# Seven quarter products in place of eight for two sequences' slot sums, in an attention and soft-mixture kernel

## The chip, the cores and the metric

The kernel runs on one core of a Trainium2 chip. The metric is the device time of one execution in microseconds (us). Three runs of the kernel before took 662.78, 663.25 and 664.02 us; their median, 663.25 us, is the time before.

## The reference, cut to what matters

The input x has 4 sequences of 2048 tokens with 256 channels, all in float32. The first half is a causal linear attention (no softmax over scores) with a two-layer MLP for each of q, k and v, a layer norm, a residual and another layer norm. The second half, which the change touches, is a soft mixture of experts with 16 experts of 16 slots, so 256 slots:

```python
logits = jnp.einsum('bnd,des->bnes', x_unit * scale, mu_unit)
dispatch = jax.nn.softmax(logits, axis=1)                  # over the 2048 tokens
combine = jax.nn.softmax(logits.reshape(B, N, E * S), axis=-1).reshape(B, N, E, S)
slot_in = jnp.einsum('bnd,bnes->besd', xn, dispatch)       # the slots' sums
h = jax.nn.gelu(jnp.einsum('besd,edh->besh', slot_in, w1) + b1[None, :, None, :], approximate=False)
slot_out = jnp.einsum('besh,ehd->besd', h, w2) + b2[None, :, None, :]
out = jnp.einsum('besd,bnes->bnd', slot_out, combine)
```

For one sequence, `slot_in` is a product of a 256 x 2048 matrix (slots by tokens, the exponentials of the logits) and a 2048 x 256 matrix (tokens by channels), divided by each slot's sum of exponentials. A column of ones beside the 256 channels yields that sum, so the product's second factor is 257 wide.

## The kernel before, in words

The 8192 tokens are cut into 16 groups of 512 (`W`), four to a sequence; a group lies in SBUF as 128 partitions by 4 chunks by channels. The work of group t is in four parts: `attend(t)` (q, k, v, scores, running state; from L776 on), `norms(t)` (the two layer norms, xn, its squares; L1022), `back(t)` (logits, their row softmax, a running smallest value `mx`, since the logits are kept with the opposite sign; L1141) and `finish(t)` (the combination with the slots' outputs, the last norm, the store; L1450). After the last group of each sequence come `softmaxes` (the largest logit of each slot is found, spread over all partitions and subtracted, then exponentials; L1234) and `slots` (the slots' sums, the experts' MLP; L1338). The last sequence is treated apart, its first three groups ahead of its last.

In `softmaxes` the way from `mx` to a tile `dg` that holds each slot's largest logit on all partitions is: two transposes on TensorE (L1246), a reduce on VectorE (L1254, tile `cm`), and `spread`, that is two VectorE instructions that make diagonal matrices (L677), one matmul of ones by the diagonals (L683) and a copy by ScalarE (L1271). GpSimd then subtracts (L1282) and ScalarE takes exponentials (L1294).

In `slot_sums` (L1316) 16 matmuls, one for each chunk of 128 tokens, accumulate one half of the slots by 257 columns in a PSUM bank of tag `ps_at`; two halves make 32 matmuls for a sequence. `slots` takes the reciprocal of the last column (L1353) and scales (L1354), and goes on with transposes (L1368), the first expert layer (L1392), transposes (L1411), a gelu and the second layer (L1438). `finish` multiplies by the slots' outputs `so` (L1542).

x comes in twice: as rows (tile `row`, L315) and, from group 2 on, also by blocks of 32 x 32 straight from memory (tile `xT`, eight DMAs, L338), which a VectorE transpose of 32 x 32 blocks then turns (L787). For groups 0 and 1 TensorE transposes `row` instead (L486, eight transposes), and VectorE and ScalarE copy the results (L476, L477).

The order of instructions on each engine is fixed before the launch by a planner, `Plan.run`: each step has an estimated length, a rank (set by `plan.begin(t + something)`), and its readers and writers; the planner takes, again and again, the step that can begin earliest by its own estimates, with the delays of `LATE` between engines. Places in SBUF, PSUM and memory are given out by tag, with a fixed count for each tag. Every engine executes its list in that order, and waits where a step's input is not there yet. SyncE (SP) issues nearly all DMAs, in one list. PSUM has 8 banks: three of tag `mm`, two of `tp`, three of `at`.

Of the kernel before, what the change touches and what calls it, by code (L numbers as in the profile page):

```python
# [17 lines left out]

PIECES = ((2, False), (2, True))

CENTERS = [['ACT', 'ACT', 'ACT', 'ACT'], ['ACT', 'DVE', 'DVE', 'DVE'], ['ACT', 'ACT', 'ACT', 'ACT'], ['DVE', 'DVE', 'DVE', 'DVE'], ['ACT', 'DVE', 'ACT', 'DVE'], ['ACT', 'DVE', 'DVE', 'DVE'], ['ACT', 'ACT', 'ACT', 'ACT'], ['DVE', 'DVE', 'ACT', 'DVE']]

SUBTRACT = ['DVE', 'POOL', 'DVE', 'POOL']

TAIL = {'norms': 0, 'back': 0.3, 'softE': 1.4, 'part': 2.2, 'soft': 1.0, 'slots2': 4.6, 'fin2': [5.5, 0.3], 'slots3': 1.7, 'fin3': [2.6, 0.2], 'table': 1.0}
LAST = 2
W = G * P
# [27 lines left out]

class Plan:

    LATE = {"PE": 0.45, "DVE": 0.25, "ACT": 0.25, "POOL": 0.25, "SP": 3.5, "IN": 0.0}
    TABLE = 1.3

    PATIENCE = {"PE": 0.0, "DVE": 0.0, "ACT": 0.0, "POOL": 0.0, "SP": 1.0, "IN": 0.0}
# [19 lines left out]
        self.order[tag].append(b)  # L81
        return b

    def step(self, engine, length, emit, reads=(), writes=(), table=None, holds=()):


        s = Step(engine, length, emit, self.base + self.count, table)
        s.holds = list(holds)
        for b in holds:
            b.left += 1  # L90
        self.count += 0.01

        if any((a[0] if isinstance(a, tuple) else a).tag.startswith("ps_") for a in reads):
            s.rank -= 1.5
        for accesses, write in ((reads, False), (writes, True)):
            for a in accesses:
                b, parts = a if isinstance(a, tuple) else (a, range(a.parts))
                if b not in s.buffers:
                    s.buffers.append(b)
                    b.left += 1  # L100
                for p in parts:
                    s.before.update(b.writers[p])
                    if write:
                        s.before.update(b.readers[p])
        for accesses, write in ((reads, False), (writes, True)):
            for a in accesses:
                b, parts = a if isinstance(a, tuple) else (a, range(a.parts))
                for p in parts:
                    if write:
                        b.writers[p], b.readers[p] = [s], []  # L110
                    else:
                        b.readers[p].append(s)
        s.before.discard(s)
        s.waiting = len(s.before)
        for o in s.before:
            o.after.append(s)
        self.steps.append(s)

    def run(self):
# [25 lines left out]
        while left:  # L145
# [43 lines left out]
                    since[b.tag].append(b.last)  # L189
            for o in s.after:  # L190
                o.waiting -= 1
                seen = end + (self.LATE[e] if o.engine != e or e == "SP" else 0.0)
                o.ready = max(o.ready, seen)
                if not o.waiting:
                    ready[o.engine].append(o)
# [4 lines left out]
def _act(n, pointers=0):  # L200
    return 0.16 + 0.00083 * n + 0.093 * pointers


def _dve(n):
    return 0.155 + 0.00105 * n
# [6 lines left out]
def _pe(n):  # L212
    return max(0.22, 0.00168 * n)
# [6 lines left out]
def kernel(  # L220
# [43 lines left out]
    for tag, n, shape in (  # L264
# [3 lines left out]
        ("kT", 1, [KC, W]),  # L268
        ("vt", 1, [G, C]),
        ("kt", 1, [G, C + 1]),  # L270
        ("sT", 1, [G, P]),
        ("a", 2, [G, C]),
        ("run", 2, [C]),
# [3 lines left out]
        ("xnT", 1, [KC, W]),  # L277
        ("lg", 7, [G, ES]),
        ("mx", 1, [ES]),
        ("ct", 5, [EH, W]),  # L280
        ("dg", 1, [EH, P]),
        ("si", 1, [EH, C]),
        ("siT", 1, [KC, ES]),
# [13 lines left out]
    plan.tag(  # L297
        "bounce", [memory.tile([KC, W, P], F32, name=f"bounce_{i}") for i in range(16)], True
    )
    plan.tag("sums", [memory.tile([G, C], F32, name=f"sums_{i}") for i in range(2)], True)  # L300
    bank_places("mm", 3)
    bank_places("tp", 2)
# [5 lines left out]
    def load_x(t):  # L308
# [14 lines left out]

        plan.step("SP", {0: 2.5, 1: 6.0, 2: 4.0}.get(t, 0.5), emit, writes=[xt])
        x_tiles[t] = xt
        if t < 2:
            return


# [907 lines left out]
    def softmaxes(groups, before=None):  # L1237
# [22 lines left out]
        if before:  # L1260
# [3 lines left out]
                nc.vector.tensor_tensor(less.place, cm.place, before.place, ALU.subtract)  # L1264

            plan.step("DVE", 0.3, emit, [before], [cm, less])
        row = spread(cm)
        cmb = plan.buffer("dg")
        plan.step(
            "ACT", _act(ES),  # L1270
            lambda: nc.scalar.copy(cmb.place.rearrange("p h e -> p (h e)"), row[:, :ES]),  # L1271
            [row], [cmb],
        )
        for t in groups:

            n = 1 if t == ngroups - 1 else G
# [30 lines left out]
    def slot_sums(groups, h):  # L1307
# [13 lines left out]
            plan.step("PE", _pe(C + 1), emit, [(l_tiles[t], [c]), n_tiles[t][0]], [psi])  # L1321
        return psi

    def part_sums(groups):

        kept = plan.buffer("xT", KC)
# [11 lines left out]
    def slots(groups, kept=None, less=None):  # L1338

        si = plan.buffer("si", EH)  # L1340
        for h in range(EH):
            psi = slot_sums(groups, h)
            r = plan.buffer("rc")

# [225 lines left out]
    for t in range(ngroups):  # L1570
# [5 lines left out]
        attend(t)  # L1576
        plan.begin(t + (TAIL["norms"] if last else 0.6))
        norms(t)
        plan.begin(t + 0.3)
        load_x(t + 2)  # L1580
        plan.begin(t + (TAIL["back"] if last else 1.1))
        back(t)
        if t == ngroups - 2:

# [5 lines left out]
            kept = part_sums(early)  # L1590
        if t % NG == NG - 1:
            groups = [t] if tail == 2 else list(range(t - NG + 1, t + 1))
            plan.begin(t + (TAIL["soft"] if tail == 2 else 1.4))
            _, less = softmaxes(groups, cm if tail == 2 else None)
            plan.begin(t + (1.7, TAIL["slots2"], TAIL["slots3"])[tail])
            so = slots(groups, kept if tail == 2 else None, less)


            first, by = ((2.6, 0.2), TAIL["fin2"], TAIL["fin3"])[tail]
            for i in range(NG):  # L1600
                plan.begin(t + first + by * i)
                finish(t - NG + 1 + i, so)
# [44 lines left out]
```

## Time and profile before

| | before |
|---|---|
| median of three runs | 663.25 us |
| the profiled execution's own time | 663.13 us |
| its span, first to last instruction | 661.4 us |
| busy: TensorE (PE) | 647.2 us, 98% |
| busy: VectorE (DVE) | 490.9 us, 74% |
| busy: GpSimd (POOL) | 298.5 us, 45% |
| busy: ScalarE (ACT) | 266.1 us, 40% |
| mean granted TensorE clock | 0.996 |
| DMA traffic | 84.71 MB, mean 128 GB/s |

The profile is of one execution. A line of the groups names the source line, the engine, the operation, output and inputs, the shapes and the count; then busy time in us and the mean of one in ns; then the engine's idle time just before, with who ended it. One float32 matmul of the program appears as two records (x256 for 128 matmuls), while a transpose appears as one. The mean of one matmul record contains latency that overlaps with the next; how long a row of them occupies TensorE is read from the chain of work that ended last, where consecutive records are merged, or from the start times of consecutive pieces. PEld is the weight load, a second record beside each matmul record. Between the first and last instruction of TensorE the only waits are some short ones in the first 65 us and near the end; after its last matmul another 7.6 us pass until the end of the span.

### The profile page before, as it was taken

What the parts mean: (1) busy time and instruction counts of PE and PEld (TensorE: products, weight loads), DVE (VectorE), ACT (ScalarE), POOL (GpSimd) and SP (SyncE); (2) the same over time, 40 slices, a digit from 0 to 9 for tenths busy, and PEclk for the clock granted to TensorE, in tenths of its full rate; (3) what the DMA queues carried; (4) which work ended last, traced back from release to release, by engine and by line L of the source; (5) the groups of instructions that cost most, each with busy time, mean ns of one, the idle gap of its engine ahead of it and who ended that gap; (6) DMA issues with size and microseconds to landing.
All of it is one profiled execution on the core that took longest, in us unless ns stands there. A gap on an engine that the chain in (4) does not pass through costs nothing.

```text
span 661.4 us, 9366 instructions
## 1 busy us (share of the span) xinstructions
PE 647.2 (98%) x2972; PEld 483.3 (73%) x2972; DVE 490.9 (74%) x1294; ACT 266.1 (40%) x597; POOL 298.5 (45%) x346
## 2 busy tenths in 40 slices
PE   9999999999999999999999999999999999999995
PEld 6657586777768877758686887776767768887874
DVE  1438586979797878778796388996978489886486
ACT  3130515333346227221516323634153544545475
POOL 4343616060739514353426605546061937646234
PEclk9999999999999999999999999999999999999998
DMA  8953655777577095836676525994677372621274
GB/s 247 261 123 109 129 96 130 126 152 158 99 158 128 15 199 174 188 87 128 127 130 136 87 68 91 238 212 104 109 152 133 65 160 70 83 65 32 33 160 160
DMA packets 322233, 84.71 MB, mean 128 GB/s; under 512 B 253068, under 2 KB 319944, under 8 KB 322184
## 3 DMA queue, kind: packets, MB, share of 16 engines
q1 hardware_dynamic: 321080, 83.06, 59.7%
q10 hardware_dynamic: 960, 0.80, 0.4%
q8 instruction: 23, 0.38, 0.2%
q0 software_dynamic: 144, 0.26, 0.1%
q14 instruction: 26, 0.21, 0.1%
HBM read 52.05 MB, written 32.04 MB: 127 GB/s over the span
## 4 chain that ended last, share of the span: by engine, by line
PE 92%; DVE 5%; issue 1%; POOL 1%; POOLq 0%; ACT 0%; DVEq 0%; ACTq 0%
PE mm L802 25%; PE at L904 8%; PE mm L1171 8%; PE mm L852 8%; PE at L1316 8%; PE at L1542 7%; PE at L987 7%; PE mm L825 7%; PE at L877 4%; PE at L991 4%; PE at L937 1%; PE at L461 1%; PE tp L486 1%; DVE xn L1096 1%; PE mm L683 1%
## 5 line engine op out<-in xcount | busy, mean ns | idle before, releaser
L812 ACT ACTIVATE hid<-mm,cols_sb 128x512 f32<-128x512 f32 x96 | 65.1, 686 | 142.1 <-PE mm L802 141.5
L542 POOL TENSOR_TENSOR root<-ve,nhalf 128x4 f32<-128x4 f32 (+1 forms) x39 | 40.7, 1044 | 125.1 <-DVE ve L1037 51.2
L987 PE MATMUL at<-state,hid 128*128 128x256 f32 x240 | 61.6, 379 | 0.0
L904 PE MATMUL at<-vt,kt 128*128 128x256 f32 x240 | 61.3, 385 | 0.0
L825 PE MATMUL mm<-both_sb,hid 128*128 128x257 f32 x256 | 59.5, 381 | 1.4 <-DVE kt L835 1.4
L802 PE MATMUL mm<-xT,W1v_sb 128*128 128x512 f32 x128 | 59.5, 593 | 0.7 <-DVE both_sb L770 0.7
L802 PE MATMUL mm<-xT,W1q_sb 128*128 128x512 f32 x128 | 59.5, 595 | 0.3 <-DVE xT L476 0.3
L1542 PE MATMUL at<-so,ct 128*128 128x256 f32 x256 | 57.9, 381 | 0.8 <-DVE row L1550 0.6
L1316 PE MATMUL at<-row,lg 128*128 128x257 f32 x256 | 58.2, 380 | 0.0
L1171 PE MATMUL mm<-mu_sb,xnT 128*128 128x256 f32 x256 | 58.1, 379 | 0.0
L852 PE MATMUL mm<-W2v_sb,hid 128*128 128x256 f32 x256 | 58.0, 379 | 0.0
L802 PE MATMUL mm<-xT,W1k_sb 128*128 128x512 f32 x128 | 57.7, 593 | 0.0
L825 PEld LDWEIGHTS mm<-both_sb,hid 128*128 128x128 f32 x256 | 48.2, 190 | 9.7 <-DVE kt L835 2.0
L1542 PEld LDWEIGHTS at<-so,ct 128*128 128x128 f32 x256 | 48.0, 190 | 9.9 <-issue 1.7
L1171 PEld LDWEIGHTS mm<-mu_sb,xnT 128*128 128x128 f32 x256 | 48.4, 190 | 8.4 <-issue 1.5
L987 PEld LDWEIGHTS at<-state,hid 128*128 128x128 f32 x240 | 45.6, 190 | 11.8 <-issue 5.7
L1030 POOL TENSOR_TENSOR row<-row,rows_sb 128x1024 f32<-128x1024 f32 x16 | 35.0, 2186 | 42.4 <-DMA row<-in_x_dram 33.9
L852 PEld LDWEIGHTS mm<-W2v_sb,hid 128*128 128x128 f32 x256 | 48.5, 190 | 6.7
L1221 POOL TENSOR_TENSOR sum<-sum,ss 128x4 f32<-128x4 f32 x16 | 4.0, 248 | 109.4 <-DVE ss L1217 92.9
L1316 PEld LDWEIGHTS at<-row,lg 128*128 128x128 f32 x256 | 48.1, 190 | 7.2 <-issue 0.4
L904 PEld LDWEIGHTS at<-vt,kt 128*128 128x128 f32 x240 | 44.4, 190 | 12.0 <-issue 5.4
L946 ACT COPY cs<-at 128x256 f32<-128x256 f32 (+1 forms) x16 | 5.9, 371 | 109.1 <-PE at L937 97.5
(150 smaller groups left out, 1250.8 us busy)
## 6 DMA issues: line engine op xcount, KB each, us to landing
bounce<-xn SPq DMA_DIRECT2D x30, 512.0 KB
row<-in_x_dram SPq DMA_DIRECT2D x16, 512.0 KB
ct<-bounce SPq DMA_DIRECT2D x64, 128.0 KB
bounce<-kt SPq DMA_DIRECT2D x30, 256.0 KB
kT<-bounce SPq DMA_DIRECT2D x60, 128.0 KB
out_dram<-row SPq DMA_DIRECT2D x15, 512.0 KB
xT<-in_x_dram SPq DMA_DIRECT2D x112, 64.0 KB
xnT<-bounce SPq DMA_DIRECT2D x56, 128.0 KB
```

What stands on the lines that cost most here:

```text
L542: nc.gpsimd.tensor_tensor(r[:, :n], v[:, :n], nhalf.to_broadcast([P, n]), ALU.pow)
L802: nc.tensor.matmul(ph.place, wa[f"W1{n}"][:, k, m * P : (m + 1) * P], xT[:, k, :], start=(k == 0), stop=(k == KC - 1),)
L812: nc.scalar.activation(hid[n][:, m, :], ph.place, AF.Gelu, bias=cols_sb[:, 4 * i + m : 4 * i + m + 1],)
L825: nc.tensor.matmul(pk[:, : C + 1], hid["k"][:, k, c * P : (c + 1) * P], wqk_sb[:, k, :], start=(k == 0), stop=(k == KC - 1),)
L852: nc.tensor.matmul(pv[:, j * C : (j + 1) * C], hid["v"][:, k, (c0 + j) * P : (c0 + j + 1) * P], wa["W2v"][:, k, :], start=(k == 0), stop=( ...
L877: nc.tensor.matmul(psc[:, toks[c]], kT[:, k, toks[c]], qT[:, k, toks[c]], start=(k == 0), stop=(k == KC - 1),)
L904: nc.tensor.matmul(pds[:, m * C : (m + 1) * C], kt[:, c, m * P : (m + 1) * P], vt[:, c, :], start=True, stop=True,)
L987: nc.tensor.matmul(po[:, :C], qT[:, k, toks[c]], s[:, k, :], start=(k == 0), stop=False,)
L1030: lambda: nc.gpsimd.tensor_tensor(row[:, :, :C], row[:, :, :C], lnb_r, ALU.add),
L1171: nc.tensor.matmul(pl[:, j * ES : (j + 1) * ES], xnT[:, k, (c0 + j) * P : (c0 + j + 1) * P], mu_sb[:, k, :], start=(k == 0), stop=(k == KC ...
L1316: nc.tensor.matmul(psi[:, : C + 1], lg[:, c, h * P : (h + 1) * P], row[:, c, :], start=(i == 0), stop=(i == n - 1),)
L1542: nc.tensor.matmul(pc[:, :C], ct[:, h, c * P : (c + 1) * P], so_t[:, h, :], start=(h == 0), stop=(h == EH - 1),)
```

## The change

In words, with line numbers of the kernel after where it has new lines:

- `pair_sums` replaces the two calls of `slot_sums` for the first two sequences. Tokens are taken in pairs of chunks (two pairs for each group), slots and channels each in halves, and the four products of quarters for a pair of chunks, which are eight matmuls of 128 (or 129) columns each, become seven by the Strassen-Winograd scheme. Eight elementwise instructions for each group (on 128 x 256 or 128 x 258 elements) form sums and differences of the quarters: five on GpSimd, three on VectorE. The seven products accumulate over all 16 chunks in seven places of three PSUM banks, both of tag `tp` and one of `at`. At the end ScalarE copies one product and seven VectorE instructions in a row combine the rest. The sums lie in one new tile `sa` and one new tile `sb`.
- `softmaxes` of the first three sequences writes `cm` to memory by a DMA (`mins`) and reads it back onto all partitions by a second DMA, instead of `spread` and the copy.
- Group 1's x is loaded by blocks (eight more DMAs and a block transpose on VectorE) in place of TensorE's eight transposes and two copies.
- `ct`, the tile of the transposed combine weights, has four places instead of five.
- The planner's constants change: `LATE` of SP from 3.5 to 4.0, the rank of steps that read PSUM from -1.5 to -0.8, several `begin` offsets by 0.1 or 0.2. In the last two sequences some centring steps go from ScalarE to VectorE or back (two more on VectorE in sum), and the order of engines for the last group's four subtractions changes.

Since the planner lays out everything anew, the order on every engine differs between the kernels from the start on.

```diff
-    LATE = {"PE": 0.45, "DVE": 0.25, "ACT": 0.25, "POOL": 0.25, "SP": 3.5, "IN": 0.0}
+    LATE = {"PE": 0.45, "DVE": 0.25, "ACT": 0.25, "POOL": 0.25, "SP": 4.0, "IN": 0.0}
...
-            s.rank -= 1.5
+            s.rank -= 0.8
...
+        ("sa", 1, [3, 2, P]),
+        ("sb", 1, [4, 2, P + 1]),
...
-        ("ct", 5, [EH, W]),
+        ("ct", 4, [EH, W]),
...
-        if t < 2:
+        if t < 1:
             return
...
+        if groups[-1] < ngroups - 4:
+            mins, cmb = plan.buffer("mins"), plan.buffer("dg")
+            plan.step(
+                "SP", 0.6,
+                lambda: nc.sync.dma_start(
+                    out=mins.place.rearrange("h p -> p h"), in_=cm.place
+                ),
+                [cm], [mins], late=4.5,
+            )
+            plan.step(
+                "SP", 0.5,
+                lambda: nc.sync.dma_start(
+                    out=cmb.place, in_=mins.place.partition_broadcast(P)
+                ),
+                [mins], [cmb],
+            )
+        else:
+            row = spread(cm)
...
+    def pair_sums(groups):
+        pa, pb, pd = plan.buffer("ps_tp"), plan.buffer("ps_tp"), plan.buffer("ps_at")
...
+            work_ = (
+                (TEES[0], lambda b_=b_, sb=sb: (sb[:, 0], b_(0, 1), b_(0, 0), ALU.subtract)),
+                (TEES[1], lambda b_=b_, sb=sb: (sb[:, 1], b_(1, 1), sb[:, 0], ALU.subtract)),
+                (TEES[2], lambda b_=b_, sb=sb: (sb[:, 2], b_(1, 1), b_(0, 1), ALU.subtract)),
+                (TEES[3], lambda b_=b_, sb=sb: (sb[:, 3], sb[:, 1], b_(1, 0), ALU.subtract)),
+                (ESSES[0], lambda a_=a_, sa=sa: (sa[:, 0], a_(0, 1), a_(1, 1), ALU.add)),
+                (ESSES[1], lambda a_=a_, sa=sa: (sa[:, 1], sa[:, 0], a_(0, 0), ALU.subtract)),
+                (ESSES[2], lambda a_=a_, sa=sa: (sa[:, 2], a_(1, 0), sa[:, 1], ALU.subtract)),
+                (ESSES[3], lambda a_=a_: (a_(0, 1), a_(0, 0), a_(0, 1), ALU.subtract)),
+            )
...
+                    for i, (a, b) in enumerate((
+                        (lg[:, u0, lo], row[:, u0, b0]), (lg[:, u1, lo], row[:, u1, b0]),
+                        (sa[:, 2, q], row[:, u1, b1]), (lg[:, u1, hi], sb[:, 3, q]),
+                        (sa[:, 0, q], sb[:, 0, q]), (sa[:, 1, q], sb[:, 1, q]),
+                        (lg[:, u0, hi], sb[:, 2, q]),
+                    )):
+                        nc.tensor.matmul(
+                            p_(i + 1), a, b,
...
+            for dst, x, y, op in (
+                (0, 4, 2, ALU.add), (5, 4, 6, ALU.add), (6, 5, 7, ALU.add), (7, 5, 5, ALU.add),
+                (1, 7, 3, ALU.add), (2, 6, 4, ALU.subtract), (3, 6, 5, ALU.add),
+            ):
+                nc.vector.tensor_tensor(c_(dst), c_(x), p_(y), op)
...
+        pairs = pair_sums(groups) if groups[-1] < ngroups - 2 * NG else None
...
-            plan.begin(t + (TAIL["soft"] if tail == 2 else 1.4))
+            plan.begin(t + (TAIL["soft"] if tail == 2 else 1.5))
...
-            plan.begin(t + (1.7, TAIL["slots2"], TAIL["slots3"])[tail])
+            plan.begin(t + (1.8, TAIL["slots2"], TAIL["slots3"])[tail])
```

The engines of the eight sums are given by `ESSES, TEES = ('POOL', 'POOL', 'DVE', 'POOL'), ('DVE', 'DVE', 'POOL', 'POOL')`. Counted over the whole kernel, TensorE's list loses 64 matmuls of 257 columns (L1316), three of 256 columns (L683) and eight transposes (L486), and gains 112 matmuls of 129 columns. VectorE's list loses six diagonals (L677) and one copy (L476) and gains 24 sums, 14 combinations of 129 columns and one block transpose. GpSimd's list gains 40 sums. SP's list gains 14 DMAs.

## The prediction

> **What bounds the kernel now.** I read the page first, for the engines' busy shares, then the chain of work that ended last in order of time, then TensorE's waits, and last the stretches in which a sequence ends. The page's first part:
>
> ```profile
> PE 647.2 (98%) x2972; PEld 483.3 (73%) x2972; DVE 490.9 (74%) x1294; ACT 266.1 (40%) x597; POOL 298.5 (45%) x346
> ```
>
> TensorE is busy nearly throughout. A busy share alone proves little, so I look at what TensorE waited for, in the view of waits restricted to it; this is the whole list:
>
> ```profile
> PE at L461 <- POOL ident masks.py:199: 1.4, 1, 1.4
> PE mm L825 <- DVE kt L835: 1.4, 1, 1.4
> PE at L937 <- DVE vt L863: 1.0, 1, 1.0
> PE mm L683 <- DVE dg L677: 0.8, 2, 0.5
> PE mm L802 <- DVE both_sb L770: 0.7, 1, 0.7
> PE at L1542 <- DVE row L1550: 0.6, 1, 0.6
> PE mm L802 <- DVE xT L476: 0.3, 1, 0.3
> PE at L1542 <- DVE so L1447: 0.2, 1, 0.2
> ```
>
> That is 6.4 us in all. So the span is TensorE's work, plus 6.4 us of waits, plus 7.6 us behind its last matmul. Work taken from TensorE shortens the kernel, as long as the instructions that then stand at its head have their inputs. The chain gives the prices (start, duration, what):
>
> ```profile
> 199.01 1.78 PE at L877 x16
> 209.85 13.92 PE at L1316 x64
> ...
> 574.08 0.87 PE tp L486 x8
> ```
>
> L1316 is the slots' sums of one sequence: 32 matmuls of 257 columns in 13.92 us, 0.435 us each. L877 is 8 matmuls of 128 columns with a fresh weight load each, 1.78 us, so 0.2225 us each.
>
> **The change, part by part.** TensorE first.
>
> The seven products: 7 matmuls x 2 pairs x 4 groups is 56 a sequence, of 129 columns. By L877 one is 0.2225 x 129/128 = 0.2243 us, so 12.56 us against 13.92: 1.36 us less a sequence, 2.72 for two. A rule of the Trainium skill speaks against this. "TensorE: Matmul & The Clock Gate", section "Back-to-back issue gap", says that the spacing of weight-load and matmul pairs is set by both, and gives about 81 ns at 128 columns but only 131 at 512: narrow matmuls would cost far more per column. Taken on a line between the two, 256 columns are 98 ns, and with two records a matmul the change would trade 64 x 98 ns for 112 x 81, 45% more, or 6.2 us more a sequence at this kernel's scale (an estimate from that page). The rows disagree: L877's record takes 111 ns and L1316's 217.5, so half the columns cost half the time here with a weight load beside each. I take the row. The nearest doubt is L877's busy time in the groups (31.2 us over 256 records, 122 ns): with that, 56 matmuls take 13.7 us and the gain is 0.2 a sequence. The chain's number is that of an undisturbed row, and L1316's own group shows the same inflation (58.2 us over 256 against 217.5 ns), so I keep 1.36, with 0.2 as lower end.
>
> The largest logits by memory: three matmuls of 256 columns leave TensorE (the chain has L904 x4 at 0.86, so 0.43 each): 1.29 us. Group 1 by blocks: eight transposes leave, 0.87 us by the L486 row of the chain. At that place TensorE waited 0.35 us for L476 and 0.30 for the diagonal L677. The first is gone. The second stays: TensorE now has four W1q matmuls (3.43 us) between the end of L704 at 33.5 and L683, arrives at 36.9, and the diagonal was there at 37.1; a further block transpose on VectorE (1.24 us, L787) stands before it, so I allow 0.5. Net there 0.1 to 0.2 us won.
>
> Sum for TensorE: 2.72 + 1.29 + 0.87 + 0.15 = 5.0 us less (with the doubt, 2.7).
>
> Now what is new for the others. VectorE: the row of such sums between two SBUF tensors is L1193, median 422 ns, mean 499, longest 1509. Twelve sums a sequence are 5.1 us, seven combinations of 129 columns out of PSUM are 7 x 0.30 by L888 (301 to 352 ns for 128 columns): 2.1 us; two diagonals go (0.55 us undisturbed). GpSimd: 20 sums a sequence at 0.73 (L971, 128x256, median 728) are 14.6 us, 16 with the 70 ns between its instructions. Neither is the bound over the span; what counts is the sequence's end. The stretches there, two of 60 us:
>
> ```profile
> 180.00:240.00 60.00, 59.87 (x311) 45.71 (x310) 48.73 (x117) 25.52 (x55) 31.99 (x28) 1.00 0.61 117
> 340.00:400.00 60.00, 60.00 (x310) 45.53 (x309) 41.06 (x109) 22.05 (x45) 22.28 (x20) 1.00 0.52 103
> ```
>
> After the stretch's length come PE, PEld, DVE, ACT and POOL. VectorE goes from 48.7 to about 55 of 60 us in the first and from 41.1 to 48 in the second; GpSimd from 32 to 48 and from 22 to 38. It fits, but TensorE is kept busy only if the planner's order holds. `sa` and `sb` have one place, so each group's sums wait for the last product of the group before, and the order of the changed kernel shows the other work that covers each: between the products of groups 0 and 1 TensorE has L877's eight, two matmuls of 512 and a state product, 4.8 us; GpSimd has five sums, 5 x 0.80 = 4.0 us, plus hand-overs, so 0.6 us of slack. Between groups 1 and 2 the cover is 9.0 us; GpSimd has there, besides five sums, two passes of 128x1024 (L1106, 2.2, and L1114, 2.4), a square-root group (2.7) and two sums of 0.73, and by my count the last sum comes just as TensorE arrives, give or take 0.5. Between 2 and 3 the cover is 6.9 us; the five sums (4.0) stand there behind two sums of 0.73 and two powers of 1.0, some of which can run earlier. Before group 0 there is plenty: 29.9 us of TensorE work between the transposes L1246 and the first product, against reduce, two DMAs, four subtractions (9.7 us), exponentials and sums, about 25 to 28. Here lies the change's weak place in SP's list: the read-back of `mins` stands behind the write, four loads of `ct` (2.5 us), a store of xn and eight loads of xT (5.4 us). A landing of such small transfers is between 1.4 us (L952 to L957) and 4.3 (L957 to L971 at 195). That cover holds; if it did not, each us late would be a us of TensorE, since all behind it queues in order.
>
> VectorE and GpSimd also get in each other's way. The row that shows it is L1014, VectorE with two SBUF tensors, in the view of that line:
>
> ```profile
> L1014 DVE SCALAR_TENSOR_TENSOR a<-a,mv,rows_sb x64: 473/479/2347, 53.3 to 584.5; 128x256 f32<-128x256 f32 x64
> ```
>
> In 180 to 240 its mean is 811 ns, while GpSimd is at 53%; its long cases (1.60 us at 205.9, 1.83 at 55.3) lie under 2.2 us GpSimd passes. Forty more GpSimd instructions, of 0.73 us, delay such an instruction by less than that, but more often. The planner's lengths hold nothing of this. For the six gaps between groups I bound the new waits of TensorE from nothing to 1.5 us each and take 0.25, near the waits that TensorE shows now (mostly 0.2 to 1.4 us, and rare): 1.5 us in all. Could they be less than nothing? The old waits at L825 (1.4, VectorE held up under GpSimd) and L937 (1.0) may vanish or grow in the new order: plus or minus 1.5.
>
> At no cost: the end of the pair sums (copy 0.3, seven combinations 2.1, reciprocals and scales 1.3: 3.9 us with hand-overs) lies beside 5.6 us of logits and state products; without them it would be bare. The eight added x loads hold SP for 4.4 to 8.5 us (the eight of L338 at 45.6 and at 6.5) ahead of the first store of kt, but sixteen b2 loads (8.7 us) move behind kT's loads, so kT is not later; TensorE needs it at 47. Four places of `ct`: SP already stood 16.7 us once for a free one (L527 behind L1542); what queues behind it are stores and loads of rows that wait for the same combination; 0 to 1 us. Two centrings to VectorE (0.41 each, 0.59 on ScalarE) and the last subtractions' engines: within 0.3 us either way, as the 16 combinations behind the last expert layer, and the 7.6 us after them, are as before.
>
> Sum: 663.13 - 5.0 + 1.5 = 659.6 for the profiled execution, which lies 0.12 under the median of the runs; so 659.7, say 659.5.
>
> **Rivals.**
>
> No new waits. The order holds as it did before (6.4 us of waits in 661), and the wait at L825 goes too: 663.2 - 5.0 - 1.0 = 657.2. For it: the planner's lengths agree with the rows (0.74 for 0.73, 0.43 for 0.42). Against: the small slack. 18%.
>
> The products are as dear as the doubt has it, or the gaps take 0.6 us each instead of 0.25: 663.2 - 2.7 + 1.5 = 662.0, or 663.2 - 5.0 + 3.6 = 661.8. 16%, most of it still a gain; a little is within 0.2%.
>
> The other side: VectorE saturates at the first sequence's end. To the 55 us come delays under GpSimd: some 40 instructions with two SBUF tensors, each 0.1 to 0.2 us later than now, 4 to 8 us, so 59 to 63 of 60. Then score masks, states and sums come late, and TensorE, in order, waits: about 4 us a group's end at the first sequence, 2 at the second plus the 1.5 of before: 663.2 - 5.0 + 7.5 = 665.7. It decides from 5.0 us of waits on. For it: 811 ns at L1014, and VectorE's 81% now. Against: TensorE lost 0.13 us between 180 and 240 although GpSimd was busy 11.9 of 12 us from 202 to 214. 10%.
>
> **How the numbers follow.** The likeliest case, 658 to 661.2, has 56%. The range from 656.7 to 662.5 leaves out some 6% below and 12% above. A measurement of this kernel can tell 0.2%, 1.3 us, from no change: faster is below 661.9. From the cases: faster 0.82, same 0.09, slower 0.09.
>
> **What would show it.** Right: the new products at 0.224 us each in the chain (12.6 us a sequence), TensorE's busy time down by about 5 us, its waits up from 6.4 to about 8, with new entries of the products behind GpSimd's sums of `sa` and `sb`. Wrong: products at 0.24 or more; a long wait of the first product for an exponential or for `dg` (SP's list); waits for masks and states in 200 to 240 with VectorE near 100% (the slow rival).

## The result, and the profile after

The changed kernel takes 685.74 us (median of 4 runs, 682.99 to 689.66), the kernel before, beside it on the same chip, 663.01 us. The ratio is 1.0353, with a 95% interval of 1.0326 to 1.0381: about 23 us slower, where 659.5 us was forecast. The profiled execution took 686.12 us, with a span of 684.4 us and a mean granted TensorE clock of 0.986 (before: 661.4 us and 0.996). The changed kernel's line numbers are 6 higher than those of before up to the softmaxes, and more behind them. One execution of the first experiment, 691.62 us, counts as slow and is left out of its median.

The page's first part, for the changed kernel:

```profile
PE 650.0 (95%) x3054; PEld 485.6 (71%) x3054; DVE 517.8 (76%) x1328; ACT 263.8 (39%) x593; POOL 328.9 (48%) x386
```

TensorE was to lose 5 us of work. It is busy 2.8 us longer than before, and its share of the span has fallen from 98% to 95%. Its list of waits (what waited, for what, total us, times, longest), without the six entries of 1.3 us and less:

```profile
PE tp L1491 <- DVE si L1477: 3.6, 1, 3.6
PE mm L1177 <- DVE xnT L540: 2.9, 1, 2.9
PE mm L808 <- DVE kt L841: 2.7, 1, 2.7
PE mm L1177 <- DVE vt L869: 2.6, 1, 2.6
PE at L883 <- DVE kT L540: 2.2, 1, 2.2
PE mm L831 <- DVE kt L841: 2.2, 1, 2.2
PE at L910 <- DVE vt L869: 2.1, 1, 2.1
PE mm L808 <- ACT hid L818: 1.8, 1, 1.8
PE at L467 <- POOL ident masks.py:199: 1.4, 1, 1.4
```

The whole list makes 26.3 us in place of 6.4. The new products, L1406, are not in it. Nearly every long wait is for VectorE, in steps that the change does not touch: keys, values, the transposed xn, the last sequence's slots.

Now the chain, for the prices that the forecast used:

```profile
191.09 3.45 PE mm L1177 x16
199.91 1.78 PE at L883 x16
...
219.30 3.60 DMA xnT<-bounce
...
223.02 1.26 DVE xnT L540
...
224.32 5.37 PE mm L1177 x16
...
235.62 1.34 PE tp L1406 x12
236.96 0.22 PE at L1406 x2
```

Seven products, 14 records, take 1.34 + 0.22 = 1.56 us, so 0.223 each: the price of the forecast, 0.2243. The wait of 2.9 us before 224 ends with a load: xnT lands at 222.9, VectorE transposes it, and only then can TensorE go on. Behind it the same 16 records of L1177 take 5.37 us in place of 3.45 at 191. The stretches of the two sequence ends, and the first 3.4 us behind that wait, show how much is lost (length; then PE, PEld, DVE, ACT, POOL busy; granted clock, DMA share, GB/s):

```profile
180.00:240.00 60.00, 54.91 (x247) 40.13 (x246) 43.35 (x108) 22.90 (x45) 26.68 (x25) 0.97 0.66 117
340.00:400.00 60.00, 54.73 (x231) 40.09 (x230) 46.97 (x114) 22.84 (x50) 30.44 (x28) 0.97 0.64 109
220.00:240.00 20.00, 17.14 (x85) 12.39 (x84) 13.11 (x32) 9.57 (x17) 13.64 (x11) 0.91 0.55 120
...
224.29:227.70 3.41, 3.38 (x8) 2.75 (x9) 0.55 (x1) 0.99 (x1) 3.41 (x2) 0.50 0.87 139
```

TensorE, which lost 0.13 us in the first stretch before and nothing in the second, loses 5.1 and 5.3 us now. Behind the wait its granted clock is 0.50 for 3.4 us, which makes 0.91 of the whole 20 us: L1177 alone took 1.92 us more. Before the last matmul the trace has five such stretches of 3.41 us at 0.50, at 63.9, 224.3, 391.5, 500.8 and 620.2 us; the kernel before has none there. TensorE is busy for 16.5 us of them, so they cost about 8 us. The sum of the time says the same: 684.4 = 650.0 busy + 26.3 waits + 8.1 at the end, and with all the forecast's savings at full clock the busy time would be 642.2, which is 7.8 us less. So: 5 us won, 20 us of new waits, 8 us of slower work behind them.

What VectorE waited for at the first end stands in SP's list. After, then before (start, us in issue, what):

```profile
199.04 0.37 SPq L1277 DMA_DIRECT2D mins<-cm  x1
199.52 8.32 SPq L533 DMA_DIRECT2D ct<-bounce  x4
...
215.94 0.49 SPq L1284 DMA_DIRECT2D dg<-mins  x1
216.47 3.39 SPq L533 DMA_DIRECT2D xnT<-bounce  x4
```

```profile
198.61 2.47 SPq L527 DMA_DIRECT2D ct<-bounce  x4
...
208.52 3.04 SPq L527 DMA_DIRECT2D xnT<-bounce  x4
```

The write of `cm` is 256 pieces of 4 bytes. Behind it the four `ct` loads take 8.3 us to issue in place of 2.5, and xnT's loads start 8 us later. The trace's records of single DMA pieces show the hold-up too: the 4-byte pieces take 9 ns each, but in the `ct` loads behind them 38 pieces of 128 bytes take 0.8 to 2.4 us each, where from 196 to 216 us of the kernel before no piece of 128 bytes takes longer than 0.19. Why they stand is not shown. VectorE, in order, stands at the `ct` transpose with the keys behind it, and GpSimd waits for the read-back:

```profile
POOL lg L1305 <- DMA dg<-mins: 20.5, 3, 11.8
```

And some of VectorE's instructions have grown; after (two lines), then before (busy us, mean ns, idle before):

```profile
L1053 DVE SCALAR_TENSOR_TENSOR row<-a,root,row 128x256 f32<-128x256 f32 x64 | 45.6, 717 | 4.2 <-POOL root L548 4.2
L1388 DVE TENSOR_TENSOR sb<-row,sb 128x258 f32<-128x258 f32 x8 | 8.6, 1074 | 1.0 <-ACT row L662 0.3
```

```profile
L1047 DVE SCALAR_TENSOR_TENSOR row<-a,root,row 128x256 f32<-128x256 f32 x64 | 30.8, 483 | 1.6 <-POOL root L542 1.6
```

VectorE's new sums, forecast at 0.42 us, take 0.87 to 1.07 us on average (medians 0.62 to 0.87). The line of the forecast's contention argument, L1014 (now L1020), has a median of 477 ns (479 before) and has not grown; what stretches L1053 is not shown.

To place the losses I use the start of the scores' matmuls of the 6th, 10th and 14th group (L877 before, L883 after; k counts from 0), the span's end, and the differences from the kernel before in each stretch, from the profiled executions. Positive is slower.

| kernel | to k=5 | k=5 to 9 (first end) | k=9 to 13 (second end) | k=13 to the end |
|---|---|---|---|---|
| before, us | 198.85 | 159.56 | 158.57 | 144.42 |
| after | +0.9 | +6.3 | +8.1 | +7.7 |

Nearly two thirds are lost at the two ends in which there are products, a third in the third end and the last sequence, where only the write of `mins`, the constants and `ct`'s places are new. Each row of such a table is one execution, and the changed kernel's four lie between 682.99 and 689.66 us, so a difference of 3 or 4 us between two stretches can be chance.

### The profile page after: what moved, and what is told of

Read it like the earlier page. It is cut to its first block, busy times and chain, and to the rows that moved or that the text cites. A ratio compares the mean times of both kernels' runs of the same rounds, so it can differ in the third digit from the quotient of the medians.

```text
span 684.4 us, 9640 instructions
## 1 busy us (share of the span) xinstructions
PE 650.0 (95%) x3054; PEld 485.6 (71%) x3054; DVE 517.8 (76%) x1328; ACT 263.8 (39%) x593; POOL 328.9 (48%) x386
## 4 chain that ended last, share of the span: by engine, by line
PE 79%; DVE 7%; DMA 5%; SPq 4%; ACT 2%; POOL 1%; issue 1%; ACTq 0%; DVEq 0%; POOLq 0%
PE mm L808 20%; PE mm L1177 8%; PE at L1665 7%; PE at L910 7%; PE at L993 7%; PE mm L831 6%; PE mm L858 6%; PE at L883 4%; PE at L997 4%; PE at L1339 3%; PE tp L1406 3%; DVE row L1053 2%; SPq L344 2%; SPq L533 2%; DMA xnT<-bounce 2%; DMA ct<-bounce 1%
## 5 line engine op out<-in xcount | busy, mean ns | idle before, releaser
L1177 PE MATMUL mm<-mu_sb,xnT 128*128 128x256 f32 x256 | 61.4, 395 | 5.4 <-DVE xnT L540 2.9
L808 PE MATMUL mm<-xT,W1q_sb 128*128 128x512 f32 x128 | 61.5, 607 | 3.0 <-DVE kt L841 2.7
L1177 PEld LDWEIGHTS mm<-mu_sb,xnT 128*128 128x128 f32 x256 | 50.7, 199 | 16.2 <-DVE xnT L540 3.7
L831 PEld LDWEIGHTS mm<-both_sb,hid 128*128 128x128 f32 x256 | 48.4, 190 | 10.8 <-DVE kt L841 2.6
L1665 PEld LDWEIGHTS at<-so,ct 128*128 128x128 f32 x256 | 48.0, 190 | 10.2 <-DVE so L1570 2.4
L1305 POOL TENSOR_TENSOR lg<-lg,dg 128x1024 f32<-128x1024 f32 (+1 forms) x17 | 38.0, 2259 | 25.1 <-DMA dg<-mins 20.5
L1053 DVE SCALAR_TENSOR_TENSOR row<-a,root,row 128x256 f32<-128x256 f32 x64 | 45.6, 717 | 4.2 <-POOL root L548 4.2
L1210 ACT ACTIVATE xn<-lg,nrm 128x256 f32<-128x256 f32 x64 | 31.9, 500 | 42.9 <-DVE lg L1187 42.8
L894 DVE SCALAR_TENSOR_TENSOR sT<-at,kt,mask 128x128 f32<-128x128 f32 x64 | 18.1, 340 | 32.5 <-PE at L883 32.4
```

The lines of the kernel that those rows point to most:

```text
L808: nc.tensor.matmul(ph.place, wa[f"W1{n}"][:, k, m * P : (m + 1) * P], xT[:, k, :], start=(k == 0), stop=(k == KC - 1),)
L831: nc.tensor.matmul(pk[:, : C + 1], hid["k"][:, k, c * P : (c + 1) * P], wqk_sb[:, k, :], start=(k == 0), stop=(k == KC - 1),)
L1053: nc.vector.scalar_tensor_tensor(row[:, c, :C], a[:, c, :], r[:, c : c + 1], row[:, c, :C], ALU.mult, ALU.add, accum_out=mv2[:, c, 0:1] if ...
L1177: nc.tensor.matmul(pl[:, j * ES : (j + 1) * ES], xnT[:, k, (c0 + j) * P : (c0 + j + 1) * P], mu_sb[:, k, :], start=(k == 0), stop=(k == KC ...
L1305: (nc.vector if engine == "DVE" else nc.gpsimd).tensor_tensor(lg[:, c : c + n, :], lg[:, c : c + n, :], cmb.place.rearrange("p h e -> p (h ...
L1665: nc.tensor.matmul(pc[:, :C], ct[:, h, c * P : (c + 1) * P], so_t[:, h, :], start=(h == 0), stop=(h == EH - 1),)
```

## Experiments on the changed kernel

My first theory was the small write: it holds up either SP's queue or the transfers themselves. Rivals: the sums, the blocks, the new order of all engines.

**Both DMAs of mins on ScalarE's queue.** The order of all else is the same.

```
-                lambda: nc.sync.dma_start(
+                lambda: nc.scalar.dma_start(
                     out=mins.place.rearrange("h p -> p h"), in_=cm.place
...
-                lambda: nc.sync.dma_start(
+                lambda: nc.scalar.dma_start(
                     out=cmb.place, in_=mins.place.partition_broadcast(P)
```

> The kernel after, with the two DMAs of the largest logits (write of mins, read-back onto dg) issued by ScalarE's queue instead of SP's; every engine's order is otherwise the same. Theory M: the write of 256 single elements of 4 bytes holds up whatever follows it in SP's list (ct loads 8.3 us instead of 2.5, xT loads 11.4 instead of 4.4), and TensorE then waits at the ends of the first three sequences; about 14 of the 22 us come from it, so about 672 us, with those loads back at 2.5 and 4.4 us. Rival C (VectorE held up under GpSimd's many more instructions is the cause): 684 to 687. Third way, M2: the write holds up the DMA engines themselves, whatever queue it is on: 682 to 687 with the loads as slow as before.

Measured: 684.83 us, ratio 1.0317 (1.0246 to 1.0387). The `ct` loads on SP's queue, with the write on ScalarE's:

```profile
196.41 8.48 SPq L533 DMA_DIRECT2D ct<-bounce  x4
```

So it is not SP's list that stands; transfers of another queue are held up just as long.

**mins in pieces of 8 bytes.** The tile in memory is turned, so that each partition writes both its values as one piece; the subtraction reads the result with strides. The order is that of the changed kernel.

```
-    plan.tag("mins", [memory.tile([EH, P], F32, name=f"mins_{i}") for i in range(2)], True)
+    plan.tag("mins", [memory.tile([P, EH], F32, name=f"mins_{i}") for i in range(2)], True)
...
-                    out=mins.place.rearrange("h p -> p h"), in_=cm.place
+                    out=mins.place, in_=cm.place
```

> The kernel after, with mins kept partition by partition, so that the write is 128 pieces of 8 bytes instead of 256 of 4 and the read-back is contiguous; GpSimd's subtraction reads dg with a step of two. Same order on every engine. Theory M, if the number of pieces counts: half of the hold-up, 677 to 680 us. If the transposed form of 4 bytes is what is slow: as with ScalarE's queue, about 672. Rival C: 684 to 687.

Measured: 677.62 us, ratio 1.0212 (1.0192 to 1.0231); 8 us come back.

```profile
200.22 5.17 SPq L533 DMA_DIRECT2D ct<-bounce  x4
```

Half the pieces, about half of what the hold-up adds to the issue (2.7 us in place of 5.8). The size of a piece and the order of the addresses change with their number, and no run parts these. By the stretches (+1.0, +2.6 and +10.0 us) the gain is 10.8 us at the first two ends, of which 2.3 are lost again behind them.

**Diagonals everywhere, no mins.**

```
-        if groups[-1] < ngroups - 4:
+        if groups[-1] < 0:
```

> The kernel after, with the diagonals, the matmul of ones and ScalarE's copy for all sequences, so no mins at all; the planner lays out the order anew. Theory M: 670 to 674 us (14 us back, 1.3 us of matmuls more). Rival C: 683 to 687, since GpSimd's forty sums are still there. Rival P (the order that the planner finds is the cause, whatever the parts): anything, but not with short waits at the sequence ends.

Measured: 681.55 us, ratio 1.0276 (1.0255 to 1.0297). The `ct` loads take 2.5 us again, but only 4 us come back: the planner lays a new order, and the last three stretches are +4.1, +3.1 and +10.9.

**Group 1 by rows.**

```
-        if t < 1:
+        if t < 2:
```

> The kernel after, with group 1 by rows and TensorE's transposes as before; only 14 lines of TensorE's order differ. In the kernel after, the way from the scores of group 0 to those of group 1 took 32.3 us instead of 28.3. If the block load is the cause of that: 4 us back, 0.9 paid for the transposes, about 682.5 us. If it is the changed order of row loads and GpSimd's additions that the planner made for other reasons: 685 to 687.

Measured: 682.78 us, ratio 1.0285 (1.0255 to 1.0315): 3 us back, where the forecast had a gain of 0.9 from the blocks. The stretch to k=5, the only one in which the order differs from the changed kernel's, gives 0.5 of it (+0.4); the rest lies in the second end (+3.8 for +8.1). So the 3 us are not shown to be the blocks' own.

## One part alone in the kernel before

Each kernel here has one part of the change and is else the kernel before; the planner lays the order anew (with the blocks it differs up to the first end only).

**The constants alone** (LATE of SP, the rank's bonus, CENTERS, SUBTRACT, six due times).

> The kernel before with the planner's constants of after alone (LATE of SP, ranks, offsets, centring and subtraction engines). Theory P (the new constants lay out a worse order; with the largest logits by the diagonals the changed kernel still took 681.6): 668 to 675 us, with waits of TensorE in the last 100 us. Rival C (the sums of the quarters and their contention are what remains): 662 to 665.

Measured: 671.9 us, ratio 1.0126 (1.0103 to 1.0149).

**The seven products alone** (with four places for `ct`).

> The kernel before with the seven products alone (and four places of ct, which their tiles need), old constants. Theory C: 666 to 675 us, since TensorE gains 2.7 us and loses more to sums that come late. Rival P: 659 to 662, the predicted gain of 2.7 us less short waits.

Measured: 684.7 us, ratio 1.0324 (1.0301 to 1.0347).

**The logits by memory alone**, for three sequences.

> The kernel before with the largest logits by way of memory alone, for three sequences. Theory M2 (the write of 256 single elements of 4 bytes holds up the DMA engines for some 6 us, three times): 668 to 675 us, loads after the write slow as in the kernel after. Rival (only the changed kernel's full GpSimd makes it matter): 662 to 664, with the loads slow but no new waits.

Measured: 691.79 us, ratio 1.0425 (1.04 to 1.045). TensorE waits 4.4, 3.5 and 4.1 us for the keys at 217, 383 and 548 us, once behind each write.

**Group 1 by blocks alone.**

> The kernel before with group 1 by blocks alone. In the kernel after, undoing this gave 3 us back. If the cost is the part's own (eight loads of xT ahead of kt's store in SP's list, and row loads and GpSimd's additions that come later): 664.5 to 667 us. If it was the order in that kernel: 662 to 664.

Measured: 664.65 us (20 runs), ratio 1.0027 (1.0009 to 1.0045).

The four make 8.9 + 21.7 + 28.8 + 1.6 = 61 us; together they cost 23. What was seen by its parts is not a sum, since three of the four make the planner lay all engines' lists anew from the first end on or earlier. The seven products lose only 4.6 of their 21.7 us at the first two ends, and 17.7 behind them. My second theory came from this: the old order fits unusually well (6.4 us of waits), and the new order is the larger part of the loss.

## The added work in the old order

To part work from order, these kernels keep every old instruction in its old place on its engine, and add the work unread, or cut it.

**The write of cm alone**, to a memory tile that nobody reads.

```
+            if groups[-1] < ngroups - 4:
+                nc.sync.dma_start(out=apart.rearrange("h p -> p h"), in_=cm.place)
```

> The kernel before, every instruction in its old place on every engine, and one more: behind cm of the first three sequences SP also writes cm to a memory tile that nobody reads (256 pieces of 4 bytes), ahead of the ct loads, where the changed kernel has it. Nothing waits for it. If the write by itself holds up the transfers behind it (as the ct loads of 8.3 us in the changed kernel suggest), the loads issued at 198.6 us take over 7 us again, VectorE stands at the ct transpose and the time is 667 to 672 (some 8 us over the kernel before, which is what pieces of 8 bytes gave back). If the hold-up only mattered because the changed kernel's order had no slack there, the loads are as slow, but the time stays under 665.

Measured: 679.77 us, ratio 1.0236 (1.0213 to 1.026): 16 us, for three writes of 1 KB. A line of SP's list behind the write, and VectorE's waits for what it loads (0.2 us in the kernel before):

```profile
200.71 8.58 SPq L527 DMA_DIRECT2D ct<-bounce  x4
```

```profile
DVE ct L534 <- DMA ct<-bounce: 12.3, 4, 5.0
```

**Products cut.** A quarter of the products is left out, and all sums.

```
+                    for a, b in ((0, P + 1),) if i % 4 == 3 else ((0, P + 1), (P + 1, C + 1)):
+                        nc.tensor.matmul(psi[:, a:b], lg[:, c, h * P : (h + 1) * P], row[:, c, a:b],
...
```

> The kernel before with its order unchanged, but the matmuls of the first two sequences' slots cut: of every four of 257 columns three become a pair of 129 and 128 columns and one a single one of 129, so a quarter of the products is left out (the output is not the sums) and there are no sums of quarters. TensorE's work falls by 64 x 0.435 - 112 x 0.223 = 2.9 us. If a saving on TensorE comes through where the order stays, the time is 660 to 661.5 with TensorE's busy time near 644.5. If the order is so tight that the saved time becomes waits, it stays at 662.5 to 664.

Measured: 662.51 us against 663.87, ratio 0.9981 (0.997 to 0.9991).

By its page TensorE is busy 644.4 us, 2.8 less (2.9 expected); by the medians about half of that comes through as time. By the stretches shown further down, the first end is 1.4 us shorter, as forecast for a sequence, the second 0.5, and 1.1 us are lost at the end (a wait of 1.5 us in two for the last rows). The profiled span is 0.9 us shorter, the median of the runs 1.4.

**The sums alone**, unread: 40 on GpSimd, 24 and 14 combinations on VectorE.

```
+                if groups[-1] < ngroups - 2 * NG and h == 0 and c == 0:
+                    for j, engine in enumerate(("DVE", "DVE", "POOL", "POOL")):
+                        (nc.vector if engine == "DVE" else nc.gpsimd).tensor_tensor(
+                            sx[engine][:], b[(1, 3, 3, 2)[j]], b[(0, 1, 1, 0)[j]], ALU.subtract)
...
```

> The kernel before, its own instructions all in their old order, and the sums of the change as extra work: per group of the first two sequences 5 sums on GpSimd and 3 on VectorE of 256 or 258 elements, put into the lists at the group's first product, and 7 of 129 per sequence on VectorE; they write tiles that nobody reads, so TensorE waits for none of them. If VectorE and GpSimd getting in each other's way is the main cost of the change, VectorE's sums take 0.6 us and more in the middle, kt and xnT come late at the first two sequences' ends and the time is 670 or more. If it is the order that the planner lays, 663 to 666.

Measured: 688.8 us, ratio 1.038 (1.0355 to 1.0405). VectorE's sums:

```profile
L1323 DVE TENSOR_TENSOR sxDVE<-row 128x258 f32<-128x258 f32 x16 | 13.3, 829 | 0.3
L1326 DVE TENSOR_TENSOR sxDVE<-lg 128x256 f32<-128x256 f32 x8 | 7.4, 925 | 0.8
```

**All three together.**

> The three together in the old order: the unread write of cm, the cut products, the unread sums. It has nearly all the work that the change adds and takes away, but not the order that the planner makes of it (the logits still go by the diagonals, and no engine waits for the sums; a quarter of the products is left out). If the new order is the larger part of the 23 us, this is 664 to 673. If the work itself is (transfers held up, engines in each other's way), 678 to 686.

Measured: 694.31 us, ratio 1.0459 (1.0428 to 1.049). The second theory falls in this form: with the old order kept, the work costs more than the change, not less. The old order has no room made for the sums; that the planner's new order hides part of what they cost is likely, but not shown by itself.

**VectorE's sums alone, and GpSimd's alone.**

> The kernel before in its old order with VectorE's part of the unread sums alone: 24 sums of 256 or 258 elements and 14 of 129. Undisturbed they are 24 x 0.42 + 14 x 0.29 = 14 us of VectorE, at the first two sequences' ends where it is fullest. If VectorE's load alone costs, the sums take 0.42 to 0.45 us each and the time is still 672 or more. If the cost comes from GpSimd's passes over VectorE's, it is 664 to 669.

> The kernel before in its old order with GpSimd's part of the unread sums alone, 40 of 256 or 258 elements, 31 us of GpSimd. VectorE has no instruction more. If GpSimd's passes stretch VectorE's own instructions (or GpSimd's own later steps come late behind them), the time is 668 or more, and VectorE's busy time rises by some us although its list is the old one. If VectorE's load is what costs, 663 to 666.

Measured: 672.38 us, ratio 1.0129 (1.0112 to 1.0146), and 686.89 us, ratio 1.0352 (1.0337 to 1.0368). VectorE's sums alone have a median of 0.43 us, as forecast, and still cost 9 us. GpSimd's sums are the dear ones, but not by stretching VectorE: its busy time is 491.8 us, against 490.9 before. VectorE stood idle instead, behind the step that GpSimd does for the running sums, L971, which now queues behind the new sums. VectorE's wait, and GpSimd's list ahead of it:

```profile
DVE a L1002 <- POOL a L971: 18.8, 1, 18.8
```

```profile
392.75 2.34 POOL L1328 TENSOR_TENSOR sxPOOL<-lg 128x256 f32<-128x256 f32 x3
395.04 0.72 POOL L971 TENSOR_TENSOR a<-a,run 128x256 f32<-128x256 f32 x1
...
397.33 2.33 POOL L1328 TENSOR_TENSOR sxPOOL<-lg 128x256 f32<-128x256 f32 x3
399.62 1.52 POOL L971 TENSOR_TENSOR a<-a 128x256 f32<-128x256 f32 x2
```

GpSimd works here without a gap; before, the same L971 steps ran from 370 to 373 us. This holds for sums put where these kernels put them; the changed kernel's planner puts them otherwise, so these 23.5 us are no measure of what GpSimd's sums cost there.

**The unread write in pieces of 8 bytes.**

```
-                nc.sync.dma_start(out=apart.rearrange("h p -> p h"), in_=cm.place)
+                nc.sync.dma_start(out=apart, in_=cm.place)
```

> The kernel before in its old order with the unread write of cm in 128 pieces of 8 bytes in place of 256 of 4. If the number of pieces makes the hold-up, the ct loads behind it take near 5 us in place of 8.6, and the time is 669 to 673, half of the 16 us of the write of 4 bytes. If any small write costs alike, 678.

Measured: 667.73 us, ratio 1.0065 (1.0049 to 1.0082). The `ct` loads take 6.3 us; the cost is 4.4 us in place of 16: less hold-up, and most of what is left fits the slack.

**Four places for ct alone.**

```
-        ("ct", 5, [EH, W]),
+        ("ct", 4, [EH, W]),
```

> The kernel before with four places for ct in place of five, and nothing else. The planner's order changes only in the last sequence. If the waits of 4 to 5 us for hz and of 2 to 4 us for si there (seen in three of the earlier runs, in steps that the change leaves alone) come from the missing place, the time is 667 to 672. If the plan finds its way round, 663 to 665.

Measured: 672.21 us, ratio 1.014 (1.0121 to 1.0159). Nearly all of it is lost in the last sequence:

```profile
PE at L1438 <- ACT hz L1430: 4.8, 1, 4.8
...
PE at L1542 <- DVE so L1447: 2.0, 1, 2.0
```

## What is left of each in the changed kernel

**The fifth place of ct given back.** The new place lies in `sb`'s memory and is free for `ct` once the last combination has been read.

```
+                if not b.left and b.tag == "sb" and not self.order["sb"]:
+                    self.places["ct"].append(self.fifth)
```

> The changed kernel with five places for ct again, the fifth in sb's memory, handed over when the last combination of the second sequence has been read; the planner's order changes only after that. If the last sequence's loss (about 3 us from its last group on, and what the third sequence's end loses) comes from the missing place as it did in the kernel before with four places, the time is 676 to 680. If it comes from elsewhere, 683 to 687.

Measured: 687.39 us, ratio 1.037 (1.0332 to 1.0409): nothing comes back. The dear place of the kernel before is not dear here, or its return is paid for by the new order that it brings (its waits include one of 5.2 us for the last sequence's slots, where the changed kernel has 3.6).

**All three given back**: five places, pieces of 8 bytes, group 1 by rows.

> The changed kernel with the fifth place of ct, mins in pieces of 8 bytes, and x's second group by rows. If the three costs add, 685.7 - 8 - 3 - 8 = 666 to 669; the rest over the kernel before, 3 to 5 us, is then the sums' on GpSimd and VectorE. If a wait that one of them takes away comes back at another place, 671 to 677.

Measured: 678.34 us, ratio 1.0222 (1.019 to 1.0254), no better than the pieces of 8 bytes alone. The costs do not add; the rival expectation, that waits come back at another place, is what happened:

```profile
PE tp L1507 <- DVE si L1493: 5.2, 1, 5.2
PE at L916 <- DVE vt L875: 3.1, 1, 3.1
```

The stretches, again one execution each, as differences from the kernel before (us), bring the runs together:

| kernel | order | to k=5 | first end | second end | k=13 to the end |
|---|---|---|---|---|---|
| after | new | +0.9 | +6.3 | +8.1 | +7.7 |
| after, 8-byte pieces | after's | +1.6 | +1.0 | +2.6 | +10.0 |
| after, all three back | new | +0.5 | +1.9 | +0.4 | +12.3 |
| before, constants | new | +0.8 | 0.0 | +2.0 | +6.2 |
| before, four `ct` | new only in the last sequence | +0.2 | -0.2 | +1.3 | +10.2 |
| before, seven products | new | +0.5 | +1.9 | +2.7 | +17.7 |
| before, unread write | old | +1.1 | +6.0 | +5.5 | +4.1 |
| before, unread write, 8-byte pieces | old | +0.2 | +2.4 | +1.4 | +0.5 |
| before, unread sums | old | -0.2 | +13.9 | +12.3 | 0.0 |
| before, products cut | old | -0.2 | -1.4 | -0.5 | +1.1 |

At the first two ends the small write explains most: it costs 6.0 + 5.5 us by itself, and smaller numbers of pieces give 5.3 + 5.5 back. With 8-byte pieces the change still costs 3.6 us there although TensorE has 2.72 + 0.86 = 3.6 us less to do. Such a write alone costs 3.8 in the old order, so between 3 and 7 us are left to the sums and the rest; the seven products alone, without any write, lose 1.9 + 2.7 us there and save 2.72, which makes 7. In the last stretch every kernel of this table whose order differs there loses 6 to 18 us, and so does the one with the diagonals everywhere (+10.9), which has no write. The kernels that keep the old order there lose at most 4 (5 with all three parts together), and only where there is a third write; group 1 by blocks alone, whose order is the old one from the second end on, loses nothing (-0.3). So a new order in the last sequence is enough for this third of the loss, which does not come from the products; what the third write adds to it in the changed kernel is not parted. Which of the changed parts spoils it is not settled: the constants and the places of `ct` each do it alone, and giving one back does not mend it. Reverting only the constants in the changed kernel was not tried. No version that computes all the sums beat the kernel before.

## Why the prediction was wrong

Right: the products cost 0.223 us (0.2243 forecast), and their record takes 111 ns at 129 columns. The rule of the Trainium skill that was weighed there, "TensorE: Matmul & The Clock Gate", section "Back-to-back issue gap", by which they would be dearer, gives about 81 ns at 128 columns and does not fit this kernel. TensorE's saving is real where nothing else moves (2.8 us of 2.9, and 1.4 us of time). Right too, and better than forecast: the six gaps between groups. They were to cost 0.25 us each; TensorE did not wait for a product once. The forecast also named the weak place, SP's list behind the small write, and then set its cost to nothing.

Wrong, in order of size:

- "That cover holds." This is the step that failed first. It looked at how long the small transfer takes to land (1.4 to 4.3 us) and who waits for it. Its cost is what it does to the transfers behind it: four `ct` loads of 8.3 us for 2.5, on whichever queue. They release VectorE, and VectorE releases the keys. GpSimd also waited for the read-back, 20.5 us in three times. At the first end the way from the transposes to the last sum ahead of the first product took 35.0 us (198.2 to 233.2), forecast at 25 to 28 against a cover of 29.9. TensorE came at 235.5, since it had itself stood 5.1 us and lost 1.9 to the clock on its way; without that it would have been there at 228.5 (an estimate from these numbers), ahead of the sums. That the first product did not wait is luck. The cost of the write is mis-sized from 0 to about 11 us at the first two ends.
- "Within 0.3 us" for the moved constants, and "0 to 1 us" for `ct`: alone they cost 8.9 us (671.90 against 663.04) and 8.8 (672.21 against 663.37). The forecast priced the moved instructions; what costs is the order that follows from them, mostly in the last sequence. In the changed kernel that stretch loses 7.7 us.
- New waits of 1.5 us: they became 20. They were looked for at the new instructions, and lie at old ones. That the old waits "may vanish or grow", plus or minus 1.5, was the only term for that.
- The clock. The sum had no term for it. Five times TensorE worked for 3.4 us at a granted clock of 0.50, each time from within 1.2 us of the end of a wait of 2.1 to 3.6 us on: about 8 us in all, 1.9 of them behind the wait at 224.
- VectorE's sums at 0.42 us: they take 0.87 to 1.07 on average in the changed kernel.
- The blocks "at no cost": 1.6 us alone. Of the 3 us that came back without them, most lie at the second end, where neither the blocks nor the order differ.

The slow rival had the sign, not the cause. It had VectorE saturated, at 59 to 63 of 60 us of the first end; VectorE was busy 43.4 us there, less than before, and 47.0 in the second end (41.1 before). It was not full but held up, by transfers that came late. A part of the rival holds: VectorE's sums alone, unread and in the old order, cost 9 us.

## What to carry to other kernels

Before a step is moved onto a small DMA, price what that DMA does to the transfers behind it, and look at its pieces, not only at its bytes. In a kernel whose order is planned as a whole and is already tight, as this one with 6.4 us of waits, a saving of 5 us on the busiest engine can be lost to the new order alone; test the added work and the new order apart, each with the other held, and look for a lower clock behind the long waits. Parts that are measured alone do not add up where they re-lay the order.

## What the runs showed of the hardware

- A DMA write of 256 pieces of 4 bytes (1 KB) made the four `ct` loads issued behind it take 8.3 to 8.6 us in place of 2.5, on the same queue and on another one; 128 pieces of 8 bytes 5.2 to 6.5. The small pieces take 9 ns each by their records; pieces of 128 bytes behind them take up to 2.4 us, in the kernel before at most 0.19 at the same place.
- Directly after TensorE waits of 2 to 3 us, 16 records that take 3.45 us elsewhere took 5.37 (the changed kernel) and 5.41 (group 1 by rows), and in both traces the granted clock was 0.50 from 224.3 to 227.7 us.
- VectorE's sums of two SBUF tensors have medians of 0.43 us (128 x 258) and 0.43 (128 x 256) when only the old GpSimd work runs (means 0.77 and 0.51), and 0.84 and 0.76 with GpSimd's sums beside them (means 0.83 and 0.93); such a sum in the kernel before has a median of 0.42. GpSimd's sums alone left VectorE's old instructions as they were (491.8 us busy, 490.9 before).
